# Joining two pairs of key tiles by an accumulating DMA in the second layer of a graph-attention kernel

## The chip, the cores and the metric

The kernel runs on one core of a Trainium2 chip, all in float32. The metric is the device time of one execution in microseconds, as the median of several runs.

## The reference

Two attention layers over a graph of 2048 nodes, for 8 batches of 2048 x 256 numbers and one adjacency matrix. The first layer is chunked softmax attention with 4 heads. The second is this one, with `h` the normalised output of the first:

```python
q = (h @ W).reshape(B, N, H, D)                  # 4 heads of 64
e = e_src[:, :, None, :] + e_dst[:, None, :, :]  # one number a node and head each
e = jnp.where(e >= 0, e, ALPHA * e)
e = jnp.where(mask, e, NEG_INF)
attn = jax.nn.softmax(e, axis=2)
h_prime = jnp.einsum('bijh,bjhd->bihd', attn, q)
return jax.nn.elu(h_prime.reshape(B, N, H * D))  # and x is added
```

## The kernel before

The kernel has two stages. The first, some 2730 us long, is the first layer; the change does not touch it. The second is a list of 32 *passes*, one for each batch and head, k = 4 x batch + head, and each pass is 16 *rounds*, one for each tile jt of 128 keys. The order of every engine's queue is written out by hand: what a round emits stands on each engine's queue in that order, and the engines only wait for each other by semaphores.

What a round does, with the lines of the profile:

- VectorE makes the weights of the tile two rounds ahead (`begun`, `clipped`, L804): e = min(max(near, far), limit) for 128 keys x 2048 queries. `near` (L795, `nears`) is the exponential of the query's part, made by ScalarE once a pass in four banks of PSUM; there is one buffer of it, so the next pass's `near` can only be written when the last e of a pass, e(15), is made. There are five buffers of e. The first and the last tile of a pass are made in two halves.
- TensorE multiplies the weights with the keys' rows (`weigh_rows`, L815): 8 matmuls of 32 columns, which run four at a time beside each other, into the pass's accumulators `acc`.
- The softmax's denominators are sums of e over all keys, weighted by `share`. They are made by *groups* of four matmuls (`add_up_rows`, L826) into one PSUM tile. A group for every tile would be 16 a pass. So most tiles are taken in pairs, m = jt // 2. At the even tile ScalarE scales its weights by the quotient of the two shares into two tiles t of 128 x 1024 (L926), and at the odd one GpSimd adds the odd tile's weights to them (L932). One group sums the pair, with the odd tile's share, LAG = 2 rounds later. The pairs in SINGLE, 3 and 7, are not joined: each of their tiles has a group of its own. That makes 6 + 4 = 10 groups a pass.
- `due` holds what is to be summed, and when. At the end of round 15 ScalarE copies the accumulators (cT, L939) and the sums (dT, L948), and the generator `ending` is put ahead of the list `aside`.

`advance()`, called once a round but in round 13, runs a step of each generator in `aside` until one has given work to TensorE. `ending` (L839 to L878) loads the rows of x (xh, on SyncE's queue), transposes dT and cT, takes reciprocals (L848), scales (z, L858), applies elu on ScalarE (L870 to L873) and on GpSimd (z L875, xh L876: two and two instructions of about 1.3 us), and stores. `preparation(b + 1)` normalises, transposes and projects the next batch during the four passes of a batch; the last batch has nothing to prepare. It also makes `quot` (L674), the quotients of the shares of each pair, and `share`.

The tiles t share their four buffers, tag `q`. Tag `o` is a pair of buffers of the same size, which the end of the first layer uses, into passes 1 and 2.

Of the kernel before, what the change touches and what calls it, by code (L numbers as in the profile page):

```python
# [8 lines left out]
F32 = mybir.dt.float32  # L9
# [3 lines left out]
AF = mybir.ActivationFunctionType  # L13
ALU = mybir.AluOpType
PSUM = bass.MemoryType.PSUM

P = 128
# [10 lines left out]
def bcast(ap, axis, n):  # L28

    ap = ap.unsqueeze(axis)  # L30
    shape = list(ap.shape)
    shape[axis] = n
    return ap.broadcast_to(shape)
# [18 lines left out]
def layers(  # L52
# [18 lines left out]
    nc = tc.nc  # L71
    B, N, F = x.shape
    H = 4
    DH = F // H
    QB = 512
    HALF = 2 * QB
    NQB = N // QB
    NKT = N // P
# [14 lines left out]
    rest = []  # L93
# [12 lines left out]
    def heads_tile(name, tag, bufs=2):  # L106
        return big.tile([P, 2, QB], F32, tag=tag, name=name, bufs=bufs)
# [105 lines left out]
    def advance(all_of=True, mask_first=False):  # L213

        moved = all_of and tick()
        for steps_of in sorted(aside, key=lambda steps_of: mask_first and steps_of is not all_limits):
            got = next(steps_of, aside)
            if got is aside:
                aside.remove(steps_of)
            moved = moved or got is not False  # L220
            if got is None:
                if here[0] < 0:
                    aside.append(aside.pop(aside.index(steps_of)))
                break
        return moved

    def drain(until=lambda: False):
        while not until() and advance():
            pass
# [330 lines left out]
        yield True  # L560


    shared, following, near = {}, {}, []
    moments = const.tile([P, B, NKT, 2], F32, tag="moments", name="moments")
    least = const.tile([P, B, H], F32, tag="least", name="least")
# [37 lines left out]
    def preparation(b):  # L603
# [68 lines left out]

        quot = small.tile([P, NKT // 2, H], F32, tag="quot", name="quot")
        nc.gpsimd.tensor_tensor(quot, logs[:, :, 0, :], logs[:, :, 1, :], ALU.subtract)  # L674
        nc.scalar.activation(far, far, AF.Exp)
        share = small.tile([P, NKT // 2, 2, H], F32, tag="share", name="share")
        nc.scalar.activation(share, logs, AF.Exp)
        yield True
        nc.scalar.activation(quot, quot, AF.Exp)
        yield True  # L680
        if b == 0:
            following[0] = sources(held, 0, tag="q", bufs=4)
# [5 lines left out]
        for blk in range(NQB):  # L688
            q = big.tile([P, NT, F], F32, tag="kv", name="qn", bufs=12)
            for two in range(2):  # L690
                ps = sides(w, two, hTs[blk])
                n = blk * NT + 2 * two
                nc.vector.tensor_tensor(  # L693
                    q[:, 2 * two : 2 * two + 2, :].rearrange("p t (h d) -> p (t h) d", h=H),
                    ps.rearrange("p t (h d) -> p (t h) d", h=H),
                    bcast(flat[:, n : n + 2, :].rearrange("p t h -> p (t h)"), 2, DH),
                    ALU.mult,
                )
                if two == 1:
                    qn.append(q)  # L700
                if blk == NQB - 1 and two == 1:
                    shared[b] = qn, held, off_s, far, quot, flat
                yield

    def fill(qb):
# [117 lines left out]
    def add_up_rows(jt, blocks, for_sums, den, first, last):  # L823

        for blk in range(NQB):
            nc.tensor.matmul(  # L826
                den[32 * blk : 32 * blk + 32, :],
                for_sums[:, jt, :],
                blocks[blk],
                start=first,  # L830
                stop=last,
            )
# [5 lines left out]
    def ending(k, cT, dT):  # L838

        b, h = passes[k]  # L840
        xs = big.tile([P, NKT, DH], F32, tag="acc", name="xh")
        nc.sync.dma_start(xs, column(x1[b], h))
        yield True
        ps = aux().rearrange("p (c k) -> p c k", c=NT)
        for c in range(NT):
            flip(ps[:, c, :], dT[:, c * P : (c + 1) * P])
        r = small.tile([P, NT, NQB], F32, tag="inverse", name="inverse")
        nc.vector.reciprocal(r, ps.rearrange("p c (b k) -> p c b k", k=32)[:, :, :, 0])  # L848
        nc.vector.tensor_reduce(  # L849
            inverse_most[:, k : k + 1], r.rearrange("p c b -> p (c b)"), mybir.AxisListType.X, ALU.max  # L850
        )
        yield
        z = big.tile([P, NQB, NT, DH], F32, tag="c", name="z")
        for part in range(2):
            ps = aux().rearrange("p (t f) -> p t f", t=NT)
            for t in range(NT):
                flip(ps[:, t, :], cT[:, part, t * P : (t + 1) * P])
            nc.vector.tensor_tensor(  # L858
                z[:, :, :, 32 * part : 32 * part + 32].rearrange("p b t d -> p t b d"),
                ps.rearrange("p t (b d) -> p t b d", d=32),  # L860
                bcast(r, 3, 32),
                ALU.mult,
            )
            yield
        low = big.tile([P, NQB, NT, DH], F32, tag="c", name="low")
        for half in range(2):
            of = slice(2 * half, 2 * half + 2)
            xh = xs[:, half * (NKT // 2) : (half + 1) * (NKT // 2), :].rearrange("p n d -> p (n d)")
            zh, lh = (i[:, of, :, :].rearrange("p b t d -> p (b t d)") for i in (z, low))
            nc.scalar.activation(lh, zh, AF.Relu, scale=-1.0)  # L870
            nc.scalar.activation(lh, lh, AF.Exp, scale=-1.0)
            nc.scalar.activation(zh, zh, AF.Relu)
            nc.scalar.activation(xh, xh, AF.Copy, bias=-1.0)  # L873
            yield True
            nc.gpsimd.tensor_tensor(zh, zh, lh, ALU.add)  # L875
            nc.gpsimd.tensor_tensor(xh, xh, zh, ALU.add)  # L876
            yield True
        nc.sync.dma_start(column(out[b], h), xs)  # L878

    LAG = 2  # L880
    SINGLE = (3, NKT // 2 - 1)
    first_layer.close()
    second_e = ctx.enter_context(tc.tile_pool(name="second_e", bufs=5))
    psum = ctx.enter_context(tc.tile_pool(name="second_psum", bufs=1, space=PSUM))
# [6 lines left out]
    def begun(k, jt):  # L891
# [3 lines left out]
            nears(near, following.pop(k), h, shared[b][2])  # L895
        return clipped(jt, h, near, shared[b][3], jt in (0, NKT - 1))


    ready = [begun(*rounds[0]), begun(*rounds[1])]
    due, ts, acc, den, before = [], None, None, None, None  # L900
    for s, (k, jt) in enumerate(rounds):
        here[0] = len(steps) + s // 4
        b, h = passes[k]
        qn, held, off_s, far, quot, share = shared[b]
        if s + 2 < len(rounds):
            ready.append(begun(*rounds[s + 2]))
        now = ready.pop(0)
        if jt == 0:
            acc = banks("acc1")
            for_sums = big.tile([P, NKT, 32], F32, tag="sr"[k % 2], name="for_sums", bufs=1)  # L910
            nc.scalar.copy(for_sums, bcast(share[:, :, h], 2, 32))
            if h == 0 and b + 1 < B:
                aside.append(preparation(b + 1))
        if jt == (2 if k % 4 < 3 else 8) and k + 1 < len(passes):
            b1, h1 = passes[k + 1]
            drain(lambda: b1 in shared)
            following[k + 1] = sources(shared[b1][1], h1, tag="add")
        weigh_rows(jt, h, now, qn, acc)
        m = jt // 2
        if m in SINGLE:  # L920
            due.append((s, jt, [now[:, blk, :] for blk in range(NQB)]))
        elif jt % 2 == 0:
            ts = []
            for half in range(2):
                t = heads_tile("t", "q", 4)
                nc.scalar.activation(  # L926
                    t, now[:, 2 * half : 2 * half + 2, :], AF.Copy, scale=quot[:, m, h : h + 1]
                )
                ts.append(t)
        else:  # L930
            for half in range(2):
                nc.gpsimd.tensor_tensor(  # L932
                    ts[half], ts[half], now[:, 2 * half : 2 * half + 2, :], ALU.add
                )
            due.append((s + LAG, jt, [ts[blk // 2][:, blk % 2, :] for blk in range(NQB)]))
        if jt == NKT - 1:
            cT = big.tile([P, 2, QB], F32, tag="hT", name="cT", bufs=1)
            for part in range(2):
                nc.scalar.copy(cT[:, part, :], acc[part])  # L939
        for entry in [entry for entry in due if entry[0] <= s]:  # L940
            due.remove(entry)
            _, j, blocks = entry
            if j == 1:
                den = rest[0][:, 0, :]
            add_up_rows(j, blocks, for_sums, den, j == 1, j == NKT - 1)
        if jt == NKT - 1:
            dT = const.tile([P, QB], F32, tag="wk", name="dT")
            nc.scalar.copy(dT, den)  # L948
            aside.insert(0, ending(k, cT, dT))

        if jt != NKT - 3:
            advance()
    drain()


# [303 lines left out]
```

## Time and profile before

| | |
|---|---|
| median of 3 runs | 4203.39 us (4202.0 to 4207.51) |
| the profiled execution's own time | 4210.55 us |
| its span, first to last instruction | 4208.7 us |
| TensorE, VectorE, ScalarE, GpSimd busy | 97%, 75%, 57%, 78% of the span |
| second layer | from about 2730 us on, 32 passes of 40 to 57 us |

The profile is one execution. PE is TensorE's matmuls, PEld its loading of weights, DVE VectorE, ACT ScalarE, POOL GpSimd, SP SyncE; L804 is line 804 of the kernel. In lines of a timeline the columns are start, duration, engine, line, operation, tiles (written <- read) and count; in brackets stands how long the engine had been idle and what ended that. An engine is counted as busy when it computes: the issue of a DMA is not counted, though it holds the queue. Busy time on the matmul array is modelled, so its share is to be read with care.

### The profile page before, as it was taken

Reading aid. Unit: us, or ns where it says so; the run is one execution under the profiler, and the core shown is the slowest. Engines: PE = TensorE matmul, PEld = TensorE weight load, DVE = VectorE, ACT = ScalarE, POOL = GpSimd, SP = SyncE. Lnnn points to the kernel's source line nnn. Section 1 sums busy time; section 2 is a strip of 40 time slices with the busy share of each in tenths; the row PEclk is TensorE's granted clock in tenths of the full one; section 3 lists DMA queues with packets and bytes.
Section 4 is the critical chain, followed back from the end, with each engine's and each line's share of the span. In section 5 each row is a group of like instructions: output and inputs, shape, how many; then the busy total and the mean of one; then the engine's idle time right before and its main releaser. Section 6 shows DMA issues by size and latency. Waiting matters only on the chain. (4 is left out here: it accounts for less than half of the span.)

```text
span 4208.7 us, 85702 instructions
## 1 busy us (share of the span) xinstructions
PE 4067.2 (97%) x34998; PEld 1507.0 (36%) x34998; DVE 3159.1 (75%) x3526; ACT 2394.9 (57%) x3090; POOL 3263.0 (78%) x1735
## 2 busy tenths in 40 slices
PE   7999999999999999999999999889999999999998
PEld 3333333333333333333333333333333333333333
DVE  5786676666766677676677677588888988888897
ACT  5655565555565565555556556564555646555554
POOL 2577787888888888788788799777776877777687
PEclk9999999999999999999999999999999999999999
DMA  3221211112112112111211222221221222122121
GB/s 112 87 77 50 57 58 48 53 53 65 48 55 63 48 51 61 54 50 53 62 50 54 55 60 62 80 58 51 63 71 33 72 52 73 51 63 71 33 61 37
DMA packets 343235, 248.11 MB, mean 59 GB/s; under 512 B 225840, under 2 KB 293168, under 8 KB 342832
## 3 DMA queue, kind: packets, MB, share of 16 engines
q1 hardware_dynamic: 337648, 223.66, 19.6%
q0 software_dynamic: 5184, 18.88, 1.2%
q8 instruction: 277, 4.54, 0.4%
q14 instruction: 126, 1.03, 0.1%
HBM read 204.15 MB, written 36.18 MB: 57 GB/s over the span
## 5 line engine op out<-in xcount | busy, mean ns | idle before, releaser
L449 DVE SCALAR_TENSOR_TENSOR E<-big,limit 128x1024 f32<-128x1024 f32 x1024 | 1181.9, 1217 | 646.1 <-PE big L441 627.9
L742 POOL TENSOR_TENSOR add<-E 128x1024 f32<-128x1024 f32 x512 | 1203.7, 2374 | 496.1 <-PE both L461 472.7
L455 ACT ACTIVATE E<-E 128x1024 f32<-128x1024 f32 x1024 | 1055.7, 1057 | 687.8 <-DVE E L449 669.1
L804 DVE SCALAR_TENSOR_TENSOR e<-near,far,limit 128x2048 f32<-128x2048 f32 (+1 forms) x576 | 1183.0, 2107 | 94.3 <-issue 55.0
L932 POOL TENSOR_TENSOR t<-t,e 128x1024 f32<-128x1024 f32 x384 | 903.9, 2383 | 346.4 <-ACT t L926 196.0
L461 PE MATMUL both<-E,v 128*32 128x512 f32 x8192 | 993.9, 594 | 0.2
L815 PE MATMUL acc<-e,qn 128*32 128x512 f32 x8192 | 972.8, 595 | 5.3 <-DVE e L804 5.1
L441 PE MATMUL big<-qT,kT 64*128 64x512 f32 x4096 | 959.4, 606 | 14.6 <-DVE E L449 12.5
L441 PEld LDWEIGHTS big<-qT,kT 64*128 64x128 f32 x4096 | 366.2, 187 | 587.7 <-issue 419.8
L926 ACT ACTIVATE t<-e,quot 128x1024 f32<-128x1024 f32 x384 | 420.1, 1144 | 266.5 <-DVE e L804 153.1
L501 POOL TENSOR_TENSOR acc<-acc,c 128x1024 f32<-128x1024 f32 x224 | 531.2, 2371 | 4.6 <-DVE c L499 4.6
L461 PEld LDWEIGHTS both<-E,v 128*32 128x32 f32 x8192 | 294.3, 109 | 535.8 <-issue 396.7
L815 PEld LDWEIGHTS acc<-e,qn 128*32 128x32 f32 x8192 | 271.8, 110 | 496.0 <-issue 451.4
L499 DVE TENSOR_TENSOR c<-both,r 128x512 f32<-128x512 f32 x448 | 308.7, 690 | 42.3 <-PE both L461 10.6
L472 PE MATMUL big<-add,ones 128*32 128x512 f32 x2048 | 280.7, 601 | 13.9 <-POOL add L742 3.4
L826 PE MATMUL rest<-t,for_sums 128*32 128x512 f32 x1536 | 211.0, 594 | 22.2 <-DVE z L858 9.5
L479 ACT COPY s<-big 128x512 f32<-128x512 f32 x256 | 149.8, 585 | 71.1 <-PE big L472 70.8
L826 PE MATMUL rest<-e,for_sums 128*32 128x512 f32 x1024 | 141.0, 592 | 0.0
L145 ACT ACTIVATE h<-x,off,rstd 128x256 f32<-128x256 f32 x256 | 139.2, 593 | 0.0
L154 PE MATMUL rest<-w,hT 128*32 128x256 f32 x1952 | 122.1, 392 | 10.7 <-DVE qn L693 6.6
L795 ACT ACTIVATE near<-es,off_s 128x1024 f32<-128x1024 f32 x64 | 71.6, 1119 | 106.8 <-DVE e L804 95.8
L154 PE MATMUL big<-hT,wk 128*32 128x512 f32 x1024 | 124.2, 600 | 7.0 <-ACT hT L165 5.8
(133 smaller groups left out, 3031.3 us busy)
## 6 DMA issues: line engine op xcount, KB each, us to landing
r<-inv SPq DMA_DIRECT2D x1024, 64.0 KB
x<-in_x_dram SPq DMA_DIRECT2D x96, 512.0 KB
es<-er SPq DMA_DIRECT2D x64, 512.0 KB
adj_in<-in_adj_dram SPq DMA_DIRECT2D x32, 512.0 KB
x<-o POOLq DMA_DIRECT2D x32, 512.0 KB, 3.3
xh<-x SPq DMA_DIRECT2D x32, 512.0 KB
out_dram<-xh SPq DMA_DIRECT2D x32, 512.0 KB
x<-x SPq DMA_DIRECT2D x28, 512.0 KB
```

The lines of the kernel that those rows point to most:

```text
L441: nc.tensor.matmul(ps[:, hh, :], ks[kt // NT][own, hp, (kt % NT) * P : (kt % NT + 1) * P], qs[qb][own, hp, :], start=True, stop=True,)
L449: nc.vector.scalar_tensor_tensor(e, ps, -0.5, bcast(limit[:, qb, kt, :], 1, 2), ALU.max, ALU.min)
L455: nc.scalar.activation(e, e, AF.Exp, scale=0.25 * EDGE)
L461: nc.tensor.matmul(both[part][32 * h : 32 * h + 32, :], vs[kt // NT][:, kt % NT, mine], es[h // 2][:, h % 2, :], start=first, stop=not first,)
L499: nc.vector.tensor_tensor(to[:, part, :], both[part], r, ALU.mult)
L501: nc.gpsimd.tensor_tensor(acc, acc, to, ALU.add)
L742: nc.gpsimd.tensor_tensor(both, tiles[0][hp], tiles[1][hp], ALU.add)
L804: nc.vector.scalar_tensor_tensor(e[:, of, :], near[:, of, :], far[:, jt, h : h + 1], limit[:, of, jt, :], ALU.max, ALU.min,)
L815: nc.tensor.matmul(acc[part][32 * blk : 32 * blk + 32, :], qn[jt // NT][:, jt % NT, own], e[:, blk, :], start=(jt == 0), stop=(jt == NKT - 1),
L826: nc.tensor.matmul(den[32 * blk : 32 * blk + 32, :], for_sums[:, jt, :], blocks[blk], start=first, stop=last,)
L926: nc.scalar.activation(t, now[:, 2 * half : 2 * half + 2, :], AF.Copy, scale=quot[:, m, h : h + 1])
L932: nc.gpsimd.tensor_tensor(ts[half], ts[half], now[:, 2 * half : 2 * half + 2, :], ALU.add)
```

## The change

In passes 3 to 30 the pairs 0 and 1, 3 and 4, 5 and 6 are joined into *fours*; pass 31 has the first two fours, passes 0 to 2 none. The single pairs are now 2 and 7. For a four, `head` is the first pair and `tail` the second:

- In the tail's odd round ScalarE rescales both t tiles of the head in place, by the quotient of the two pairs' odd shares (`quads`, three new columns of 128 x 4, made once a batch by three small subtractions on GpSimd and an exponential).
- GpSimd adds the odd tile to the tail's t as before, and after each of its two halves issues a DMA from its own queue that adds the head's t (128 x 1024, 512 KB) onto the tail's, in SBUF.
- The four is summed by one group, five rounds after the tail's odd round instead of two. That leaves 3 + 4 = 7 groups a pass. The last four of a pass is summed in round 2 of the next pass; dT and `ending` follow then.
- The t of pairs 3 and 6 take the buffers of tag `o`.

```diff
+    SINGLE = (2, NKT // 2 - 1)
+    FOURS = ((0, 1), (3, 4), (5, 6))
...
         nc.gpsimd.tensor_tensor(quot, logs[:, :, 0, :], logs[:, :, 1, :], ALU.subtract)
+        quads = quot[:, SINGLE[0], :], quot[:, SINGLE[1], :], low[:, :H]
+        for to, (first, second) in zip(quads, FOURS):
+            nc.gpsimd.tensor_tensor(to, logs[:, first, 1, :], logs[:, second, 1, :], ALU.subtract)
...
         nc.scalar.activation(quot, quot, AF.Exp)
+        nc.scalar.activation(quads[2], quads[2], AF.Exp)
...
-    SINGLE = (3, NKT // 2 - 1)
...
+    due, open_of = [], {}
+
+    def sum_up(until):
+
+        for entry in sorted((entry for entry in due if entry[0] <= until), key=lambda entry: entry[0]):
+            due.remove(entry)
+            _, k, j, blocks = entry
+            state = open_of[k]
+            add_up_rows(
+                j, blocks, state["for_sums"], rest[0][:, 0, :], state["left"] == state["all"], state["left"] == 1
+            )
+            state["left"] -= 1
+            if state["left"] == 0:
+                dT = const.tile([P, QB], F32, tag="wk", name="dT")
+                nc.scalar.copy(dT, rest[0][:, 0, :])
+                aside.insert(0, ending(k, state["cT"], dT))
...
+        fours = FOURS[: 0 if k < 3 else 2 if k == len(passes) - 1 else 3]
+        tail_of = {second: first for first, second in fours}
+        heads = tuple(first for first, _ in fours)
...
         elif jt % 2 == 0:
             ts = []
             for half in range(2):
-                t = heads_tile("t", "q", 4)
+                t = heads_tile("t", "o", 2) if fours and m in (3, 6) else heads_tile("t", "q", 4)
                 nc.scalar.activation(
                     t, now[:, 2 * half : 2 * half + 2, :], AF.Copy, scale=quot[:, m, h : h + 1]
                 )
                 ts.append(t)
         else:
+            if m in tail_of:
+                for t in pairs_of[tail_of[m]]:
+                    nc.scalar.activation(t, t, AF.Copy, scale=quads[heads.index(m - 1)][:, h : h + 1])
             for half in range(2):
                 nc.gpsimd.tensor_tensor(
                     ts[half], ts[half], now[:, 2 * half : 2 * half + 2, :], ALU.add
                 )
-            due.append((s + LAG, jt, [ts[blk // 2][:, blk % 2, :] for blk in range(NQB)]))
+                if m in tail_of:
+                    nc.gpsimd.dma_start(ts[half], pairs_of[tail_of[m]][half], accum_op=ALU.add)
+            pairs_of[m] = ts
+            if m not in heads:
+                wait = LAG + 3 if m in tail_of else LAG
+                due.append((s + wait, k, jt, [ts[blk // 2][:, blk % 2, :] for blk in range(NQB)]))
...
-        for entry in [entry for entry in due if entry[0] <= s]:
-            due.remove(entry)
-            _, j, blocks = entry
-            if j == 1:
-                den = rest[0][:, 0, :]
-            add_up_rows(j, blocks, for_sums, den, j == 1, j == NKT - 1)
-        if jt == NKT - 1:
-            dT = const.tile([P, QB], F32, tag="wk", name="dT")
-            nc.scalar.copy(dT, den)
-            aside.insert(0, ending(k, cT, dT))
-
+            open_of[k]["cT"] = cT
+        sum_up(s)
         if jt != NKT - 3:
             advance()
+    sum_up(len(rounds) + LAG + 3)
     drain()
```

More of the change, by code (lines that the diff above doesn't have):

```diff
@@ L701, in preparation @@
                 if blk == NQB - 1 and two == 1:
-                    shared[b] = qn, held, off_s, far, quot, flat
+                    shared[b] = qn, held, off_s, far, (quot, quads), flat
                 yield
@@ L896, in begun @@
         return clipped(jt, h, near, shared[b][3], jt in (0, NKT - 1))
+    due, open_of = [], {}
[12 more added lines that the diff above has]
+                aside.insert(0, ending(k, state["cT"], dT))
     ready = [begun(*rounds[0]), begun(*rounds[1])]
-    due, ts, acc, den, before = [], None, None, None, None
+    acc, ts, pairs_of = None, None, {}
     for s, (k, jt) in enumerate(rounds):
@@ L903, in layers @@
         b, h = passes[k]
-        qn, held, off_s, far, quot, share = shared[b]
+        qn, held, off_s, far, (quot, quads), share = shared[b]
         if s + 2 < len(rounds):
@@ L911, in layers @@
             nc.scalar.copy(for_sums, bcast(share[:, :, h], 2, 32))
+            n = NKT // 2 + len(SINGLE) - len(fours)
+            open_of[k] = {"for_sums": for_sums, "left": n, "all": n}
             if h == 0 and b + 1 < B:
@@ L920, in layers @@
         if m in SINGLE:
-            due.append((s, jt, [now[:, blk, :] for blk in range(NQB)]))
+            due.append((s, k, jt, [now[:, blk, :] for blk in range(NQB)]))
         elif jt % 2 == 0:
```

## The prediction

> **What bounds the kernel now.** I read the engine totals of the page first, then the second layer cut into its passes, then one pass on VectorE, ScalarE and GpSimd. The page's first section:
>
> ```profile
> PE 4067.2 (97%) x34998; PEld 1507.0 (36%) x34998; DVE 3159.1 (75%) x3526; ACT 2394.9 (57%) x3090; POOL 3263.0 (78%) x1735
> ```
>
> TensorE is nearly always busy, so fewer matmuls look like time won. That average must be read by pass. I cut the trace at the copies of cT (L939), one window for each of passes 24 to 30 (engine columns PE, PEld, DVE, ACT, POOL; the last three numbers are clock, DMA share, GB/s):
>
> ```profile
> 3844.10:3890.70 46.60, 44.02 (x400) 14.70 (x396) 41.67 (x25) 29.14 (x43) 36.93 (x20) 1.00 0.38 108
> 3890.70:3933.50 42.80, 42.09 (x400) 14.20 (x396) 36.62 (x24) 27.17 (x39) 33.25 (x16) 1.00 0.20 42
> 3933.50:3986.00 52.50, 51.27 (x576) 19.31 (x568) 44.50 (x36) 22.63 (x31) 33.80 (x19) 1.00 0.13 32
> 3986.00:4027.70 41.70, 40.62 (x384) 14.77 (x388) 36.70 (x22) 21.88 (x26) 33.33 (x16) 1.00 0.21 57
> 4027.70:4068.10 40.40, 39.09 (x352) 13.95 (x348) 37.97 (x23) 21.90 (x26) 33.30 (x16) 1.00 0.20 52
> ```
>
> The first four windows are one batch, in which the next batch is prepared: 183.6 us, and TensorE is idle for 5.6 us of them. It sets the pace. The fifth is a pass of the last batch, without preparation. There VectorE never pauses except once, before e(0):
>
> ```profile
> 4034.10 0.25 DVE L848 RECIPROCAL inverse<-rest 128x16 f32<-128x16 f32 x1
> 4034.47 2.34 DVE L804 SCALAR_TENSOR_TENSOR e<-near,far,limit 128x2048 f32<-128x2048 f32 x1
> ...
> 4040.18 25.05 DVE L804 SCALAR_TENSOR_TENSOR e<-near,far,limit 128x2048 f32<-128x2048 f32 x12
> 4067.63 4.73 DVE L804 SCALAR_TENSOR_TENSOR e<-near,far,limit 128x1024 f32<-128x1024 f32 x3 [2.39 <-issue]
> ```
> ```profile
> 4065.27 2.27 ACT L795 ACTIVATE near<-es,off_s 128x1024 f32<-128x1024 f32 x2 [3.50 <-DVE e L804]
> ```
>
> The pause is ScalarE's `near` for the next pass, for which there is one buffer. 38.0 us of work and 2.39 us of pause are the whole pass of 40.4 us, so VectorE sets these passes, and matmuls saved there are worth nothing. GpSimd in the same pass:
>
> ```profile
> 4049.49 1.30 POOL L875 TENSOR_TENSOR z<-z,low 128x512 f32<-128x512 f32 x1
> 4050.87 1.29 POOL L876 TENSOR_TENSOR xh<-xh,z 128x512 f32<-128x512 f32 x1
> 4052.11 14.12 POOL L932 TENSOR_TENSOR t<-t,e 128x1024 f32<-128x1024 f32 x6
> ```
>
> Six adds in a row without a gap: from pair 4 on GpSimd just keeps up. The only DMA that the kernel's GpSimd queue issues regularly is the store of the first layer, 512 KB like the new ones:
>
> ```profile
> L554 POOL DMA_DIRECT2D x<-o x32: 797/842/967, 277.7 to 2816.3; - x32
>   POOL o L553: 9.2, 31
> DMA to landing us min/median/max: 3.2/3.3/6.4
> ```
>
> It holds the queue for 0.84 us, waits 0.30 us (9.2/31) for the add before it, and the next add starts 0.03 us after it: 1.17 us for each.
>
> **The change part by part.**
>
> *Removed.* Passes 3 to 30 have three groups of sums less, pass 31 two: 86 groups. In a full stretch groups follow each other every 0.86 us (4172.02 to 4172.87), so TensorE loses 74 us of work, 2.58 us a pass.
>
> *Added on ScalarE.* Each four rescales the head pair's two halves, 6 x 1.10 us = 6.6 us a pass (L926 takes 2.20 us for two). ScalarE is 22 to 29 us busy in a pass and has the room, but its queue is in order, and here is the point: the rescaling of pair 5 for pair 6 is emitted in round 13, `near` of the next pass in round 14. So `near`, and all of VectorE's next pass behind it, now waits until GpSimd has finished pair 5's adds. Before, `near` waited for VectorE alone.
>
> *Added on GpSimd.* Six DMAs a pass, 6 x 1.17 = 7.0 us, on top of 33.3: 40.3 us. Nothing of it can be overlapped on that engine. An accumulating DMA has no row; 0.84 us is the nearest one. From below the issue is free and only the 0.30 + 0.03 us of waiting stay, from above it costs twice 0.84 because two tiles are read. I take 0.84. The Trainium skill (DMA: Bandwidth & Descriptors, SWDGE vs HWDGE) says that accumulation during a DMA is for GpSimd's queue only, so the issue could not go to SyncE; no run here shows that.
>
> *Moved.* The single pair is 2 instead of 3, and the last four is summed in round 2 of the next pass, so `ending` starts three rounds later: z and xh on GpSimd now stand after pair 3 and after pair 4, inside the tight half of the pass (the order of the changed program shows it). SyncE's load of xh is queued behind the loads of es; xh is used ten microseconds later, which hides it, and its cost uncovered is a few us of ScalarE's wait. The three small subtractions (0.25 us each, L674) and one exponential for each batch fall where GpSimd waits between pairs 1 and 3; uncovered they are 8 us in all.
>
> *The loop that this makes.* Everything below is in order and follows from the one before it:
> - GpSimd from e(7) on: 0.17 to start (4031.93 to 4032.10 for pair 0), pair 3 4.72, z and xh 2.62, pair 4 with its two DMAs 2 x (2.38 + 1.17) = 7.10, z and xh 2.62, pair 5 4.72: 21.95.
> - ScalarE: wait 0.1, second half of the rescaling 1.10, `near` 2.27: 3.47.
> - VectorE: wait 0.1, e(0) in two halves and e(1) 4.74 (4027.19 to 4031.93), e(2) to e(7) 6 x 2.26, inverse and most 0.43, one z 0.60: 19.43.
>
> L = 44.85 us, the least time from e(7) to the next pass's e(7), against 40.4 where nothing is prepared.
>
> *The sum.* There are 28 such loops, from pass 3 to pass 31. In a batch with preparation the four loops also hold what is queued in them: the norms on GpSimd 3.9, top, bottom, far and logs on VectorE 0.85, two qn 1.2. ScalarE's copies and norms (5.2 us more in two of the passes) compete with the rescalings there: between 0 and 10.4; I take 2, since GpSimd's own queue runs beside most of them. So 4 x 44.85 + 7.95 = 187.35 against 183.6: +3.75, six times: +22.5. TensorE needs 183.6 - 10.3 = 173.3 and is no bound on average; in the batch's third pass (52.5 - 2.6 us) it is, and I let it trail by the 4 to 5 us that the five e buffers allow. If it can't, 4.4 us a batch come on top. The last four loops: 4 x (44.85 - 40.43) = +17.7. At the end GpSimd's pair 6 is done 26.6 us after e(7), and two sums follow: 28.7 instead of the 22.8 now (4168.35 to 4191.1): +6. In all +46 on the profiled execution's own 4210.55 us; that execution is 7.2 above the median of the runs, so 4250 us as the runs are measured.
>
> *The landing.* Pair 6 takes its buffers from pair 3, whose DMAs must have landed. The second is issued 13.5 us after e(7) and the buffer is wanted at 20.95, so 7.4 us are free. Plain ones took 3.3, the slowest 6.4, and it is the store in the second layer's stretch whose packets began late. I take it as hidden.
>
> The Trainium skill (Collectives: The Full Stack, The bandwidth ceiling) says that a reducing transfer reads two sources through the same ring and runs at half the rate of a copy. By that the packets' 1.4 us would become an estimated 2.8, and the landing still just fits; no run here shows it.
>
> **Rivals.** A time within 0.2% (8.4 us) counts as no change, about what a measurement of this kernel can tell.
>
> *Faster: TensorE keeps the pace.* The three groups less come through where it is the bound: 6 x 10.3 = 62 us, 4141 us. For it speak 97% and the four batch windows. It decides where L is small enough: the change in all is 28 L - 1209.6, which is zero at L = 43.2. That needs an issue that costs GpSimd next to nothing (L = 42.5 if a DMA were entirely free: -20 us, 4184). Against it: the order of the queues, and the 0.84 us of every issue in the trace.
>
> *No change.* With the issue at its lower bound L is 43.2: 4203 us.
>
> *Much slower: the transfers land late.* Then pair 6's scaling waits, and the rescaling and `near` behind it on ScalarE. From 7.4 us after the issue on, each us costs 28, and 31 more because both rescalings then come after it: at 9 us 4325, at 12 us (twice the slowest) 4409.
>
> *TensorE can't trail and ScalarE is in the way* (10.4 and 4.4 us a batch): +50 and +26, 4326 with both.
>
> **How the numbers follow.** Forecast 4250 with 0.62, whose own range is 4212 to 4300 (issue cost up to double: +47); late landing 0.10; both stalls of the last rival 0.08; no change 0.07; faster 0.13. Faster 0.13, same 0.07, slower 0.80. The range goes from 4188, within the faster cases, to 4322, within the late landings; about a tenth is left out at each end.
>
> **What would show it.** Right: passes 28 to 30 last about 45 us each, VectorE's pause before e(0) grows from 2.39 to some 6 us or more, ended by `near`, which itself waits for the rescaled t and that for GpSimd's t; the new DMA takes about 0.84 us of GpSimd; TensorE's share falls to about 94%. Wrong: passes 28 to 30 stay near 40 us (then some step of the loop is shorter than its row), or the batch windows fall to 173 us with TensorE full (the first rival), or the scaling of pair 6 waits for a DMA (the late landing).

## The result, and the profile after

The changed kernel takes 4342.27 us, the median of 4 runs (4333.41 to 4347.68), against 4203.4 us before: 1.0325 times as long, with a 95% interval of 1.0312 to 1.0338. It is slower, as forecast, but by 139 us and not by 46, and the time lies beyond the predicted range. The profiled execution's span is 4335.8 us.

The totals, and the group of the new DMAs (busy us, mean ns | idle time of the queue before them and what ended most of it):

```profile
PE 4085.5 (94%) x34310; PEld 1469.1 (34%) x34310; DVE 3163.3 (73%) x3526; ACT 2579.3 (59%) x3270; POOL 3424.2 (79%) x1931
L965 POOL DMA_DIRECT2D t<-t x172 | 150.9, 877 | 132.9 <-ACT t L959 89.7
```

TensorE is down from 97% to 94%. The issue of an accumulating DMA holds GpSimd's queue for 0.88 us; 0.84 had been taken. But before 37 of the 172 issues the queue waited for a rescaling on ScalarE, 89.7 us in all, which the sum did not have. (GpSimd's 3424.2 us include the 150.9 of these issues: on this queue the profile counts the issue of a DMA as busy.)

The same passes as before the change, 24 to 27 (one batch) and 29, again cut at the copies of cT:

```profile
3913.00:3965.68 52.68, 45.33 (x376) 13.81 (x376) 39.36 (x24) 35.59 (x50) 43.32 (x27) 0.97 0.55 126
3965.70:4017.44 51.74, 44.59 (x369) 13.12 (x368) 38.59 (x24) 33.41 (x46) 39.16 (x23) 0.97 0.49 103
4017.40:4069.44 52.04, 50.70 (x544) 19.36 (x544) 45.63 (x36) 29.21 (x39) 41.44 (x30) 0.97 0.59 127
4069.50:4113.32 43.82, 39.70 (x364) 12.22 (x364) 36.49 (x22) 28.02 (x33) 35.82 (x21) 1.00 0.41 89
4163.50:4212.14 48.64, 41.60 (x324) 12.03 (x324) 38.30 (x23) 28.39 (x34) 38.67 (x23) 0.93 0.51 109
```

This batch takes 200.3 us instead of 183.6 (187.35 was forecast), and pass 29 takes 48.6 instead of 40.4 (44.85). The third window, in which TensorE is fullest, is nearly unchanged (52.5 to 52.0 us); the second of the batch and pass 29 have grown by 8.9 and 8.2 us, the first by 6.1 and the fourth by 2.1. The DMA share (last but one) has gone from 0.13 to 0.38 before to 0.41 to 0.59.

Now pass 29 itself, on ScalarE, GpSimd, SyncE's queue and VectorE:

```profile
4160.81 2.25 ACT L801 ACTIVATE near<-es,off_s 128x1024 f32<-128x1024 f32 x2
...
4170.20 1.16 ACT L952 ACTIVATE t<-e,quot 128x1024 f32<-128x1024 f32 x1 [3.40 <-DVE e L810]
4175.02 1.15 ACT L952 ACTIVATE t<-e,quot 128x1024 f32<-128x1024 f32 x1 [3.67 <-DMA t<-t]
4176.76 0.59 ACT L917 COPY dT<-rest 128x512 f32<-128x512 f32 x1 [0.58 <-PE rest L832]
4177.24 2.19 ACT L959 ACTIVATE t<-t,quot 128x1024 f32<-128x1024 f32 x2
...
4201.93 1.15 ACT L952 ACTIVATE t<-e,quot 128x1024 f32<-128x1024 f32 x1 [3.64 <-DMA t<-t]
4204.61 1.15 ACT L952 ACTIVATE t<-e,quot 128x1024 f32<-128x1024 f32 x1 [1.54 <-DMA t<-t]
4206.05 1.15 ACT L959 ACTIVATE t<-t,bottom 128x1024 f32<-128x1024 f32 x1 [0.28 <-POOL t L961]
4208.39 1.15 ACT L959 ACTIVATE t<-t,bottom 128x1024 f32<-128x1024 f32 x1 [1.18 <-POOL t L961]
4209.44 2.25 ACT L801 ACTIVATE near<-es,off_s 128x1024 f32<-128x1024 f32 x2
```
```profile
4162.33 0.88 POOL L965 DMA_DIRECT2D t<-t  x1 [0.30 <-POOL t L961]
4162.94 2.66 POOL L961 TENSOR_TENSOR t<-t,e 128x1024 f32<-128x1024 f32 x1
4165.90 0.88 POOL L965 DMA_DIRECT2D t<-t  x1 [0.30 <-POOL t L961]
4168.06 7.00 POOL L961 TENSOR_TENSOR t<-t,e 128x1024 f32<-128x1024 f32 x3 [1.29 <-DVE e L810]
4178.94 0.88 POOL L965 DMA_DIRECT2D t<-t  x1 [3.87 <-ACT t L959]
```
```profile
4161.93 1.48 SPq L596 DMA_DIRECT2D es<-er  x2
4163.47 0.43 SPq L848 DMA_DIRECT2D xh<-x  x1
```
```profile
4163.14 13.77 DVE L810 SCALAR_TENSOR_TENSOR e<-near,far,limit 128x1024 f32<-128x1024 f32 x7 [6.19 <-issue]
4180.20 0.26 DVE L854 RECIPROCAL inverse<-rest 128x16 f32<-128x16 f32 x1 [3.29 <-PE rest L157]
```

Three things are to be seen. VectorE's pause before e(0) has grown from 2.39 to 6.19 us, which is the forecast step: `near` (4209.44) stands behind the rescaling of pair 5, and its second half (4208.39) waits for GpSimd's adds. And there is a second pause, which was not: the last DMA of the pass before is issued at 4165.90, and the scaling of pair 1 at 4175.02, which writes into that DMA's source, still waits for it, 9.1 us later. Behind that scaling on ScalarE stand dT and the rescaling of pair 0. So TensorE's transposes of dT come late, VectorE's reciprocal waits 3.29 us for them with e(6) and e(7) behind it, and GpSimd's next DMA waits 3.87 us. Around the first of these two DMAs (4162.33) SyncE issues the loads of es and xh, 3 x 512 KB.

The third is the sign that the prediction gave for late landings: the two scalings of pair 6 (4201.93 and 4204.61) wait 3.64 and 1.54 us for DMAs. Here that costs nothing, because the rescaling behind them still has to wait for GpSimd.

### The profile page after: what moved, and what is told of

It is laid out like the page before. It is cut to its first block, busy times and chain, and to the rows that moved or that the text cites. A ratio compares the mean times of both kernels' runs of the same rounds, so it can differ in the third digit from the quotient of the medians.

```text
span 4335.8 us, 84744 instructions
## 1 busy us (share of the span) xinstructions
PE 4085.5 (94%) x34310; PEld 1469.1 (34%) x34310; DVE 3163.3 (73%) x3526; ACT 2579.3 (59%) x3270; POOL 3424.2 (79%) x1931
## 5 line engine op out<-in xcount | busy, mean ns | idle before, releaser
L821 PE MATMUL acc<-e,qn 128*32 128x512 f32 x8192 | 1050.7, 615 | 81.8 <-ACT for_sums L935 55.2
L961 POOL TENSOR_TENSOR t<-t,e 128x1024 f32<-128x1024 f32 x384 | 932.5, 2446 | 161.7 <-DVE e L810 112.6
L965 POOL DMA_DIRECT2D t<-t x172 | 150.9, 877 | 132.9 <-ACT t L959 89.7
L832 PE MATMUL rest<-t,for_sums 128*32 128x512 f32 x848 | 149.9, 611 | 56.9 <-DMA t<-t 47.1
L959 ACT ACTIVATE t<-t,quot 128x1024 f32<-128x1024 f32 x116 | 126.5, 1138 | 1.6 <-POOL t L961 1.6
```

Of the source, the lines that this page charges most:

```text
L821: nc.tensor.matmul(acc[part][32 * blk : 32 * blk + 32, :], qn[jt // NT][:, jt % NT, own], e[:, blk, :], start=(jt == 0), stop=(jt == NKT - 1),
L832: nc.tensor.matmul(den[32 * blk : 32 * blk + 32, :], for_sums[:, jt, :], blocks[blk], start=first, stop=last,)
L961: nc.gpsimd.tensor_tensor(ts[half], ts[half], now[:, 2 * half : 2 * half + 2, :], ALU.add)
```

## The experiments

Where only one execution was made, its time is compared with the 4201 to 4210 us of before's runs; ratios with intervals stand where more were. One kernel below was run on two occasions, and its executions lie between 4182.3 and 4188.8 us, so a few us between single executions say little. L, as in the prediction, is the time from e(7) to the next pass's e(7), which is the length of passes 28 to 30. Landing is the time from a DMA's issue to its last packet.

**Which four costs.** First the third four is left out:

```diff
-        fours = FOURS[: 0 if k < 3 else 2 if k == len(passes) - 1 else 3]
+        fours = FOURS[: 0 if k < 3 else 2]
```

> Passes 3 to 31 join only pairs 0+1 and 3+4; pairs 5 and 6 stay pairs. My theory: the third four does the harm (it puts GpSimd's adds of pair 5 ahead of the next pass's near, and its DMAs land beside the loads of es, where pair 1 of the next pass, dT and then e(6) wait for them). Then passes 28 to 30 go back to about 40.4 us, each batch of four passes saves 4 x 1.72 us of TensorE (183.6 to about 177), and the whole is about 4160 us (4140 to 4185), below the kernel before. Rival A, any four costs GpSimd's time: two thirds of the loss stay, about 4295 us. Rival B, a DMA that accumulates disturbs the other engines: likewise about 4295 us.

4286.93 us, ratio 1.0195 (1.0178 to 1.0212): my theory's 4160 was far off, and the 4295 of both rivals close. The transfers landed in 4.1 to 4.4 us (medians), and still the passes took 45.5 to 46.8 us:

```profile
POOL t L961 <- ACT t L952: 229.4, 35, 11.4
ACT t L952 <- DMA t<-t: 185.2, 57, 6.4
...
DVE e L810 <- POOL t L961: 92.2, 37, 4.3
```
```profile
4158.76 1.15 ACT L952 ACTIVATE t<-e,quot 128x1024 f32<-128x1024 f32 x1 [3.88 <-DMA t<-t]
4162.37 1.15 ACT L952 ACTIVATE t<-e,quot 128x1024 f32<-128x1024 f32 x1 [2.46 <-DMA t<-t]
4163.42 2.25 ACT L801 ACTIVATE near<-es,off_s 128x1024 f32<-128x1024 f32 x2
```

The first lines are waits of the second layer (us in total, times, longest), the others ScalarE in pass 29. Even a landing that nothing disturbs is waited for: pair 6 takes the buffers of pair 3, and with no rescaling of pair 5 behind it, `near` follows directly on its scaling, 1.1 us after VectorE's last e (4162.30). VectorE waits for GpSimd's adds to give buffers of e back. So any four costs time here, and not the third only. Next the third four alone:

```diff
+        fours = FOURS[2:] if 3 <= k < len(passes) - 1 else ()
...
```

> Passes 3 to 30 join only pairs 5+6. My theory: near still waits for the rescaled pair 5 and pair 1 still waits for the late DMA; only GpSimd's two DMAs of pair 4 (2.3 us) leave the loop: passes 28 to 30 about 45 to 46 us, 4280 to 4320 us in all. Rivals A and B: a third of the loss, about 4250 us, passes 28 to 30 about 43 us.

4281.09 us, inside the theory's 4280 to 4320, though passes 28 to 30 took 48.5, 47.7 and 45.1 us where 45 to 46 was expected. Its two transfers landed after 6.3 and 9.2 us (medians). Two fours cost 82 us and the third alone 76, all three together 139: the costs overlap and can't be added.

**The loads of es.** They start when `near` is done, so they meet the third four's DMAs. In this kernel they are left out from pass 5 on:

> The changed kernel without the loads of es from pass 5 on (an old es is used again, so the weights are those of another batch or head). My theory: the DMAs of the third four land in 4 to 5 us like the others, instead of 8 to 9; passes 28 to 30 fall from 48 to 50 us to the 44.9 that the loop of the prediction gives, and the whole by some 90 to 130 us, to 4210 to 4250. If the slow landing comes from GpSimd or from the accumulation itself, landing and time stay (4340).

4263.42 us, 79 us less than the change, though a little above the 4210 to 4250 expected. All landings are now 4.1 to 4.4 us (medians), and passes 28 and 29 show the forecast loop:

```profile
4051.80:4096.47 44.67, 39.03 (x324) 10.96 (x324) 38.01 (x23) 28.31 (x33) 38.72 (x23) 0.96 0.47 95
4096.50:4141.57 45.07, 40.09 (x324) 13.08 (x324) 38.19 (x23) 28.31 (x33) 38.72 (x23) 0.92 0.46 94
```

The forecast was 44.85 us and 187.35 us for a batch; five of the six batches here take 187.5 to 187.7, the last one 189.4. Then the same bytes, later:

```diff
-        if jt == (2 if k % 4 < 3 else 8) and k + 1 < len(passes):
+        if jt == 13 and k + 1 < len(passes):
```

> The change as it is, with the loads of es queued in round 13 of a pass instead of round 2, behind the store of the pass before; no byte less. Theory (what the third four lands late for is that the es loads are in flight at the same time): the es loads start about 17 us after e(7) and land before near, the third four then has only the load of xh beside it and lands after 4.2 to 6 us; passes 28 to 30 take 45 to 46 us, 4262 to 4300 us. Rival (the amount of traffic in a pass is what counts, not its time): 4342 us within 10.

4307.19 us, 7 above the upper edge, but far from the rival's 4342. Passes 28 to 30 took 45.7 to 45.9 us, as expected. The third four's landings fell to 5.8 and 4.8 us (medians). But `near` now waits for the loads of es themselves, 26 times and 29.3 us in all. So it is when the loads run that counts, more than how many bytes they are; this place for them is only half a repair.

**Copying instead of accumulating.**

```diff
-                    nc.gpsimd.dma_start(ts[half], pairs_of[tail_of[m]][half], accum_op=ALU.add)
+                    nc.gpsimd.dma_start(ts[half], pairs_of[tail_of[m]][half])
```

> The six DMAs copy instead of accumulating, so that half of each four's values is lost; the same bytes are written from the same queue at the same places. Theory (the third four's landing of 8 to 9 us is the accumulating packets beside the loads of es and xh): the issue stays at 0.84 to 0.88 us, the packets take 0.16 us instead of 0.33, the third four lands after 5 to 6 us, passes 28 to 30 take 45 to 46.5 us, 4265 to 4300 us. Rival (what is late is the issue and the queue, whatever the packets do): landing and time stay, 4342 us within 10.

4270.98 us, in the theory's range. A packet takes 0.159 us instead of 0.328. Transfers that meet no loads land after 2.55 us, the third four after 5.0 and 7.2 us, and passes 28 to 30 take 44.4 to 44.9 us, as without the loads of es: landings of 5.0 and 7.2 us, though late beside the loads, cost almost nothing.

**Without the DMAs.** The line of the DMA is deleted, the rescalings stay.

> The six DMAs of a pass are left out, so that the sums of rows are too small; the rescalings and the order of everything else stay. Theory (GpSimd's time for the issues, and the landings of the third four, are what the change costs beyond its order): GpSimd's arc loses 2 x 1.17 us, the loop is 42.5 us in passes 28 to 30, and 28 x 2.35 come off the 4263 us of the run without the es loads: about 4200 us. Rival (the rescalings in ScalarE's queue, ahead of the next pass's near, are the cost, and the transfers are only late because of them): passes 28 to 30 stay at 45 us or above, 4260 us or more.

4189.87 us, 10 below the theory and far from the rival:

```profile
4040.20:4082.34 42.14, 38.42 (x324) 10.30 (x324) 38.00 (x23) 28.15 (x34) 33.20 (x17) 1.00 0.20 50
```

L is 42.1 us, against the 42.5 that the prediction gave for free DMAs. Without its DMAs the change is faster than the kernel before, but no faster than the move of the single pair alone (below: 4183.6).

**`near` and the rescalings.** If `near` standing behind the rescaling of pair 5 is what makes the loop, then moving that rescaling and its DMAs behind `near` should free it. Here that is done, without the later es loads ("the run before" in the text is that kernel):

> As the run before, and the rescaling of pair 5 and both DMAs onto pair 6 are put behind near of the next pass. My theory: with both causes gone VectorE's pause before e(0) is 2.4 us again, passes 28 to 30 take 41 to 43 us, and TensorE's saving shows: 4150 to 4190 us, below the kernel before. If near behind the rescaling is not a cause: as the run before, 4210 to 4250.

4258.31 us: a miss. Passes 28 to 30 took 43.2 to 46.4 us. The DMAs from pair 5 to 6 now start later, back to back, the second lands after 7.1 us, and pair 1's scaling waits for its buffers instead. One wait took the other's place. Without the rescalings altogether:

> The change without the later loads of es (the first batch's are used again) and without the rescalings of the heads, so that the sums carry wrong weights; the six DMAs and every other instruction stay. Theory (of the 73 us that the DMAs cost without the collision, most come through the rescaling of pair 5 ahead of near): near waits for VectorE alone, GpSimd's 33.3 + 7.0 = 40.3 us are just as long as VectorE's pass, and passes 28 to 30 take 40.5 to 42.5 us: 4190 to 4225 us. Rival (GpSimd's time in the queue is the cost, whoever waits for it): passes 28 to 30 stay at 44.5 to 45 us, 4263 us within 10.

4222.43 us, inside the theory's 4190 to 4225, with passes 28 to 30 at 41.5, 43.0 and 42.0 us. So 41 of the 4263.4 us go when the rescalings go. The 32.5 us that are left above the run without DMAs (4189.9) are not GpSimd's time alone: in this run too ScalarE's scalings of pairs 0 and 6 wait for landings. How the rest divides was not measured.

**Other places for the fours.** If the late four is the bad one, early fours should be free. Two fours, of pairs 0, 1 and 2, 3, with single pairs 4 and 7:

```diff
-    SINGLE = (2, NKT // 2 - 1)
-    FOURS = ((0, 1), (3, 4), (5, 6))
+    SINGLE = (4, NKT // 2 - 1)
+    FOURS = ((0, 1), (2, 3))
...
```

> Two fours in passes 3 to 31 as in the first experiment, but of pairs 0 and 1 and of pairs 2 and 3, with pair 4 single. Theory (the place in the pass is what costs: near must not stand behind a rescaling that waits for GpSimd's last adds, nor pair 1's buffers behind a transfer that shares the queues with the loads of es): near waits for VectorE alone again, GpSimd's 33.3 + 4 x 1.17 = 38.0 us fit in VectorE's 40.4, passes 28 to 30 take 40 to 41 us, and the third pass of each batch, which TensorE sets, gets up to 1.7 us shorter: 4185 to 4215 us. Rival (each DMA costs its time on GpSimd and its landing wherever it stands): as the other two fours, 4287 us within 15.

> The same two early fours, but only in the third pass of each batch from pass 6 on, the one of 52.5 us that TensorE sets; single pairs 4 and 7 everywhere. Theory: only these passes change, 7 of them, of which one is in the last batch; up to 1.7 us each, 4190 to 4205 us. Rival (each DMA costs wherever it stands): 7/29 of the 82 us that the two late fours cost, so 4223 us within 10.

Theory and rival missed in both: 4369.84 us, ratio 1.0389 (1.0371 to 1.0406), and 4247.75 us. VectorE in pass 29 of the first of the two:

```profile
4232.37 4.61 DVE L809 SCALAR_TENSOR_TENSOR e<-near,far,limit 128x2048 f32<-128x2048 f32 x2 [1.12 <-POOL t L960]
...
4240.88 9.25 DVE L809 SCALAR_TENSOR_TENSOR e<-near,far,limit 128x2048 f32<-128x2048 f32 x5 [3.90 <-POOL t L960]
```

It waits for buffers of e, which GpSimd's late adds still read. In the second one, passes that have no four at all are longer than before, 41.9 us instead of 40.4, so the place of the single pair was the suspect. It was moved alone, in the kernel before, `SINGLE = (4, NKT // 2 - 1)` and then `SINGLE = (2, NKT // 2 - 1)`:

> The kernel before with one number changed: the single pair in the middle of a pass is pair 4 instead of 3; no fours. Theory (in the run with early fours in the third passes only, it is this move that cost the time): GpSimd then has four pairs to add before its pause, holds the e buffers longer, and VectorE waits 1.4 us for one in every pass: 41.9 us in passes 28 to 30, 4203 + 29 to 32 x 1.5 = 4245 to 4255 us. Rival (the place of the single pair is free, the early fours cost 6 us each time): 4203 us within 6.

> The kernel before with the single pair in the middle moved to pair 2, as the change has it; no fours. Theory (pairs 3 to 6 then stand in a row before the next pass, so GpSimd runs later into it, but near does not wait for GpSimd): between 4195 and 4215 us, passes 28 to 30 within 1 us of 40.4. Rival (this move costs as much as the one to pair 4): 4250 us.

4243.58 us at 4, and 4188.83 at 2. So the move to 4 explains the second miss and about 40 of the 164 us of the first. The other 124 come with the early fours in every pass (in passes 28 to 30 VectorE waits 15.3 us for GpSimd's adds, and 4.3 with the move alone) and were not taken apart; and the move to 2, a part of the change that the prediction had priced at nothing, is a gain. It was timed once more:

> The kernel before with the single pair at 2 and no fours, timed. Theory (the single pair at 2 lets GpSimd pause earlier, so that the norms of the first pass of a batch no longer press on the pairs behind them: 46.6 us to 44.2): 4186 to 4192 us, ratio 0.996 to 0.997. Rival (chance of one execution): 4203 us within 5.

4183.62 us, ratio 0.9951 (0.9936 to 0.9966). The kernel before already had the wait that it lessens; here VectorE, in pass 24 before the change:

```profile
3869.34 13.77 DVE L804 SCALAR_TENSOR_TENSOR e<-near,far,limit 128x2048 f32<-128x2048 f32 x7 [1.41 <-POOL t L932]
3886.59 4.74 DVE L804 SCALAR_TENSOR_TENSOR e<-near,far,limit 128x1024 f32<-128x1024 f32 x3 [3.48 <-POOL t L932]
```

4.9 us in this pass; with the single pair at 2 it is 2.6, and the pass takes 44.2 us instead of 46.6. A batch takes 180.4 instead of 183.6.

**Fours only where TensorE sets the time.** That is the third pass of each batch. The change's three fours there, everything else as before:

```diff
+        fours = FOURS if k > 3 and k % 4 == 2 else ()
+        single = SINGLE if fours else (3, NKT // 2 - 1)
...
```

> The change's three fours, single pair 2 included, but only in the third pass of each batch from pass 6 on; all other passes as before. Theory: these passes are set by TensorE (52.5 us before, 51.2 without the DMAs), so GpSimd's longer loop stands beside matmuls; 1 to 2.6 us less in each of 7 passes, 0 to 3 us more in the pass behind it, where pair 1 waits for the last landing: 4190 to 4215 us. Rival (each four's DMAs cost wherever they stand): a quarter of the 138 us, 4237 us.

4185.83 us, ratio 0.9957 (0.9942 to 0.9972), better than expected: the third pass takes 49.9 us instead of 52.5, the one behind it 40.8 instead of 41.7. In these passes the single pair is at 2 as well, so this is not the fours' gain alone. Two fours, with the single pair left at 3, `FOURS = ((0, 1), (4, 5))`, and each four summed one round earlier than in the change:

> Two fours, of pairs 0 and 1 and of pairs 4 and 5, in the third pass of each batch only, with the single pair at 3 as before; nothing else moves. Theory: two groups of sums less where TensorE sets the time, 7 x 1.5 to 1.7 us, and no rescaling ahead of near that waits for the last adds: 4190 to 4197 us, faster than the kernel before. Rival (each DMA costs wherever it stands): 7 x 4 x 1.17 us more, 4236 us.

4216.88 us, ratio 1.0031 (1.0019 to 1.0043): a miss. TensorE's work in the third pass fell from 51.3 to 49.8 us, but the pass only to 52.2 or 52.3, and the next one grew from 41.7 to 43.3. This was not taken apart further. Last, the single pair at 2 everywhere, and three fours in the third pass of batches 1 to 6:

> The single pair is pair 2 in every pass, and the three fours stand only in the third pass of batches 1 to 6. Theory (the two gains add up: 15 us from the single pair's place, and TensorE's third pass 52.5 to 49.9 with 0.9 back in the pass behind it): 4165 to 4180 us, ratio 0.991 to 0.994. Rival (both gains are the same slack, counted twice): 4186 to 4190 us.

4173.18 us, ratio 0.9922 (0.9908 to 0.9935), faster than both kernels, in the middle of the theory's range. Its passes 24 to 27:

```profile
3812.70:3855.90 43.20, 43.09 (x396) 14.55 (x392) 39.88 (x24) 29.18 (x42) 36.88 (x20) 1.00 0.35 105
3855.90:3898.67 42.77, 42.06 (x400) 14.03 (x396) 37.37 (x24) 27.37 (x38) 33.32 (x16) 1.00 0.21 45
3898.70:3947.73 49.03, 48.61 (x555) 18.27 (x548) 43.61 (x35) 29.61 (x39) 39.90 (x28) 1.00 0.46 101
3947.70:3990.86 43.16, 41.86 (x388) 12.80 (x392) 38.78 (x24) 22.07 (x26) 33.27 (x16) 1.00 0.24 60
```

In the third window TensorE is busy for 48.6 of 49.0 us: there three groups less are time won, although the second DMA of the third four lands after 8.4 us. With the single pair at 2 and no fours the same pass takes 51.7 us, so the fours alone win 2.7 there, about the 2.58 of the removed groups; the pass behind it grows by 1.4 us.

## Why the prediction was wrong

**Where the 139 us come from.** Each row is a run. The fourth takes two steps at once, DMAs added and loads of es left out, because no run leaves out both; rows three and four are single executions.

| kernel | us | step |
|---|---|---|
| before | 4204.0 | |
| single pair at 2, no fours | 4183.6 | -20 |
| fours without DMAs | 4189.9 | +6 |
| with DMAs, without the later es loads | 4263.4 | +73.5 |
| the change | 4342.3 | +79 |

**The step that failed is the landing**, "I take it as hidden". The prediction asked only for pair 6's buffers, which come from pair 3, and gave them 7.4 us. It did not ask for pair 1's, which come from pair 5: their DMAs are the last of a pass, issued just when `near` ends, and the end of `near` is what lets the loads of es go. It took 3.3 us, the landing of a store, and called 6.4 the slowest; by the same measure of the profile, which runs 0.3 to 0.5 us beyond the last packet, the third four took 8.2 and 9.6 us (medians). The second landing stops ScalarE, and with it dT, the rescaling of pair 0 and VectorE's reciprocal. Three runs show the collision: the change without the es loads (-79 us), with them later (-35), and with copies (-71), whose packets take half as long everywhere, so that this run is the least pure of the three.

The rival of late landings had the right kind of cause and, at 9 us, a price of 4325, close to what came. It had one chance in ten, and that the price fits is luck: it named pair 6's buffers, and their waits were there (5.2 us in pass 29) but cost nothing there. Those buffers did hold `near` up, by 1.1 us, in the run with two fours.

**The loop was right.** From pass 29 to pass 30, disturbed as they are, e(7) ends at 4186.38, GpSimd's adds of pair 5 end at 4208.3 (21.9 us; 21.95 forecast), `near` at 4211.7, and e(1) at 4216.5: 30.1 us, where the forecast steps give 30.26. The rest of the loop, e(1) to e(7), took 18.5 us instead of 14.6, and that is the stall above. Without the collision L was 44.67 to 45.07 us, forecast 44.85, and without DMAs 42.1, forecast 42.5.

**The issue was right**: 0.88 us with 0.30 of waiting, 1.17 had been taken for both and the 0.03 behind. GpSimd's next add starts 0.61 us into the issue and takes 2.66 us instead of 2.37, so that add and DMA together take 3.56 us, 1.2 more than an add.

**The single pair's move was priced at nothing** and is worth 20 us by itself. It takes no matmul away, so TensorE did not set all four passes of a batch, as had been read from its 5.6 idle us: in the first of them VectorE waited for GpSimd. In the change this can't be seen apart; I take it that the longer loop of GpSimd, `near` and VectorE covers it, which was not tested.

**That TensorE can trail was right**: without the collision a batch took 187.6 us in the median, 187.35 forecast, though its third window alone took 51.5. The **first rival**, that TensorE keeps the pace, was wrong for the change, but right for that one pass: where the fours stand there alone, it falls by 2.7 us (51.7 to 49.0).

**What remains.** Without the collision the change takes 13 us more than the 4250 forecast. The 28 loops, from e(7) of pass 3 to e(7) of pass 31, give few of them: 1307.8 us instead of 1263.5, +44.3 where +40.2 was forecast. The rest is the end, a term that the sum had too small: from e(7) of pass 31 to the last instruction it is 56.3 us instead of 40.3, +16 where +6 was forecast. GpSimd is done with pair 6 after 26.6 us, as forecast; what follows was not taken apart.

**The rule that was weighed**, the Trainium skill's half rate for a reducing transfer (Collectives: The Full Stack, The bandwidth ceiling): this case agrees. An accumulating packet took 0.328 us and a copying one 0.159, 2.06 times, and 4.1 to 4.4 us of landing stand against 2.55. By the rule the landing "still just fits"; without the loads of es it did in the change's own loop, and not with two fours, where `near` waited for it. What it met was decisive.

## What to carry to other kernels

For a transfer between on-chip tiles, list everybody who waits for it: the reader of its target, and whoever reuses its source, in the next pass too; then look which loads the same event sets free, for they will be in flight together. An engine whose share of busy time is 97% may still set the time of only some passes: put a change that spares its work there alone, and time the small moves that a change needs (here the single pair) by themselves, since they can be worth more than the change.

## What had not been expected of the hardware

The granted clock fell in the passes with stalls. TensorE in pass 29 of the change, its two pauses and then its windows (us, busy, granted clock, DMA share, GB/s):

```profile
4164.57 7.83 PE L821 MATMUL acc<-e,qn 128*32 128x512 f32 x48 [3.73 <-ACT for_sums L935]
4175.04 0.82 PE L832 MATMUL rest<-t,for_sums 128*32 128x512 f32 x2 [2.08 <-DMA t<-t]
```
```profile
4155.00:4160.00 5.00, 5.00 (x52) 1.00 0.54 121
4160.00:4164.60 4.60, 0.86 (x10) 1.00 0.40 106
4164.60:4168.00 3.40, 3.40 (x16) 0.57 0.97 211
...
4172.00:4175.00 3.00, 0.96 (x8) 1.00 0.64 124
4175.00:4180.00 5.00, 4.96 (x24) 0.66 0.00 0
```

After a pause of 3.7 us the clock was 0.57 for the next 3.4 us, and after one of 2.1 us it was 0.66 for the next 5. With pauses of at most 1.7 us (passes 28 to 30 of the run without DMAs) it stayed at 1.00; TensorE was busy there for 38.4 us with the matmuls that take 41.6 in this pass. The Trainium skill (TensorE: Matmul & The Clock Gate, What's actually happening) gives half the clock after an idle window of about 3.4 us. The first pause agrees with that; the second is shorter, and the clock fell all the same. What this adds to the late dT was not measured by itself.

An accumulating transfer of 512 KB that lands after 4.1 to 4.4 us alone took 8 to 9 us beside 1.5 MB of loads; a copy, 2.55 alone, took 5.0 to 7.2 there.
